# Norms on ScalarE by logarithm and exponential, and some products moved to GpSimd, in a two-layer convolution and state-space kernel

## The chip, the core and the metric

The kernel runs on one core of a Trainium2 chip. A core has TensorE (matrix products; weight loads overlap them), VectorE, ScalarE and GpSimd for work on elements, and a queue of SyncE that issues the transfers here. TensorE writes its results to PSUM, eight banks of 128 x 512 float32; the other tiles lie in SBUF. In the profile the engines are called PE (PEld for weight loads), DVE, ACT, POOL and SP. The metric is the device time of one execution in microseconds, as the median of several runs; lower is better.

## The reference

The input is x, 8 images of 64 channels by 128 by 128, float32. The first layer is a filter with a weight of its own for every pixel:

```python
h = conv3x3(x, w1) + b1;  h = where(h >= 0, h, 0.2 * h)
w_lp = softmax(conv1x1(h, w2) + b2, axis=1)        # 9 weights for each pixel
x = x + sum_k tap_k(x) * (delta_center - w_lp[k])
```

The second layer takes each image as 16,384 pixels with 64 channels:

```python
x_norm = layernorm_over_channels(x) * w + b
seq = res = layernorm(x_norm) * w + b
for i in range(2):                                  # bimamba_block
    xz = rmsnorm(seq) @ in_proj;  x, z = split(xz)  # 128 channels each
    y = mamba(x, z, forward) + mamba(x, z, backward)
    seq = seq + y @ out_proj
seq = conv3x3(rmsnorm(seq)) + res
x = x + depthwise3x3(conv1x1(x_norm)) * seq
g = depthwise3x3(conv1x1(layernorm_over_channels(x)))       # 340 channels
out = x + conv1x1(gelu(g[:170]) * g[170:])
```

One direction of `mamba` makes a causal convolution over 4 pixels with SiLU (`u`), a step `dt = softplus(...)` for each of 128 channels, and vectors B and C of 16 values for each pixel. For each channel and each of 16 states it runs over the pixels `h = exp(dt * A) * h + dt * B * u`, and sums `C * h` over the states. Every norm divides by the square root of the mean square over 64 channels plus 1e-5; there are five kinds of place for it: three in the first part of the second layer, one behind each pair of directions, and one ahead of the feed-forward part.

## The kernel before

**The scan.** A chunk is 1024 pixels of one image in one layer and one direction: 8 x 2 x 2 x 16 = 512 chunks, the class `Chunk`. Its 128 channels by 16 states are 16 tiles of 128 partitions (32 channels x 4 states) by 1024 pixels. Tile u has a slot of its own, so that a chunk has 16 slots and an image 1024. In each slot ScalarE makes the decay `exp(dt * A)` into one of two PSUM buffers `w` (`decay`, L1058), VectorE runs the recurrence (`scan`, L1076 forward and L1078 backward), and the result is multiplied by C (`product`). For each pair of tiles GpSimd makes the drive `bu` = dt * u * B (`drive`, L1050), three buffers of 128 x 2048. A product is on VectorE (L1100) or on GpSimd (L1097), as `on_pool` decides by the number of the tile: GpSimd takes the even tiles but for 4 and 12, tile 8 only beside certain other work, and none where the slot before it is that of a GELU. Where GpSimd takes it, the scan writes to `hs` in SBUF, else to `w` in PSUM. `keep` (L1090) copies the last state on ScalarE. `collect` (L1109, L1116) sums over the states on TensorE.

**The other work** is laid beside the scans. `Front` (16 pieces of 1024 pixels an image) makes the first layer and three norms; `Mix` makes the 3x3 convolutions behind the scans and one norm; `Ffn` is the feed-forward part with GELU. The next image's fronts run beside this image's third and fourth direction, the last image's mix and this one's feed-forward beside the next image's scans. The chunk of a second direction adds both directions, projects, and makes one norm.

**The order** is written out by hand. `at(time, phase, fn)` puts a step into a slot and one of six phases (FEED, SCAN, MID, PROD, DECAY, REST). The sorted list is emitted in that order, and every engine runs its own instructions in the order of the list, waiting for semaphores. So a step that waits holds up all that is behind it on its engine. The slots before the first chunk's have negative numbers; `FIRST_FRONT_AT` is the first front's.

**PSUM.** Two buffers `w` take four banks; `y`, `mm` (chunks), `bg` and `acc` (fronts, mix, feed-forward) have one bank each.

**A norm** is the class `Norm` (L406 to L430), with the square `sq` at hand:

- `means`: four matmuls with `sq` as weights and `half_mean` give the mean for each pixel, pixels on partitions, 128 x 8 in PSUM
- `means_out` (L418): ScalarE copies it to SBUF and adds epsilon
- `root` (L421): GpSimd raises it to the power -1/2
- `spread` (L427): eight matmuls with the identity put it on all 64 channels of both halves, 128 x 512 in PSUM

VectorE then multiplies by it: `scaled` (L542), `third_norm` (L574), `normed` (L1162). There are 768 norms: three in each of 128 fronts, one in each of 128 pieces of the mix, one in each of 256 chunks of a second direction.

**Table loads.** ScalarE's functions lie in sets, of which one is loaded at a time. SiLU, softplus and GELU each need another set than the exponential of the decay; the loads are put in by the compiler, ahead of the first function that needs another set.

Of the kernel before, what the change touches and what calls it, by code (L numbers as in the profile page):

```python
# [8 lines left out]
F32 = mybir.dt.float32  # L9
# [26 lines left out]
PW = W + 2  # L36
FEED, SCAN, MID, PROD, DECAY, REST = range(6)
# [8 lines left out]
LAST_MIX_STEP, LAST_MIX_AT, LAST_FFN_STEP, LAST_FFN_AT = 16, 826, 8, 1084  # L46
# [9 lines left out]
def kernel(ctx: ExitStack, tc: tile.TileContext, a: dict, out: bass.AP):  # L56
# [55 lines left out]
    neg_half = const([P, 2 * ROWS], "neg_half")  # L112
    nc.vector.memset(neg_half, -0.5)
# [4 lines left out]
    half_mean = const([P, 2], "half_mean")  # L118
    nc.vector.memset(half_mean, 0.0)
    nc.vector.memset(half_mean[0:C, 0:1], 1.0 / C)  # L120
    nc.vector.memset(half_mean[C:P, 1:2], 1.0 / C)
# [42 lines left out]


# [240 lines left out]
    class Norm:  # L406


        def means(self, ps, sq):
            self.mp = ps("ms")  # L410
            for w in range(ROWS):
                nc.tensor.matmul(  # L412
                    self.mp[:, 2 * w : 2 * w + 2], sq[:, W * w : W * w + W], half_mean, start=True, stop=True
                )

        def means_out(self):
            self.r = wk.tile([P, 2 * ROWS], F32, tag="r", name="r", bufs=4)
            nc.scalar.activation(self.r, self.mp[:, 0 : 2 * ROWS], AF.Identity, bias=eps)  # L418

        def root(self):  # L420
            nc.gpsimd.tensor_tensor(self.r, self.r, neg_half, ALU.pow)  # L421

        def spread(self, ps):
            self.rb = ps("rb")
            for w in range(ROWS):
                for h in range(2):
                    nc.tensor.matmul(  # L427
                        self.rb[C * h : C * h + C, W * w : W * w + W],
                        self.r[:, 2 * w + h : 2 * w + h + 1].to_broadcast([P, C]), ident, start=True, stop=True,
                    )  # L430
# [9 lines left out]
    class Front:  # L440
# [140 lines left out]
        def plan(self, a):  # L581
# [25 lines left out]
            at(a + 23, DECAY, self.filtered)  # L607
# [14 lines left out]
            at(a + 33, REST, lambda: n2.means(acc_tile, self.sq))  # L622
            at(a + 34, DECAY, n2.means_out)
            at(a + 34, REST, n2.root)
            at(a + 36, REST, n2.spread, acc_tile)
            at(a + 37, DECAY, self.scaled, n2)
# [21 lines left out]
    class Mix(Front):  # L648
# [40 lines left out]
        def plan(self, a):  # L689
# [15 lines left out]
            at(a + 12, REST, lambda: n1.means(bg_tile, self.sq))  # L705
            at(a + 13, DECAY, n1.means_out)
            at(a + 13, REST, n1.root)
            at(a + 16, REST, n1.spread, bg_tile)
            at(a + 17, DECAY, self.scaled, n1)
            at(a + 17, DECAY, self.norm)  # L710
# [8 lines left out]
    class Ffn:  # L719
# [174 lines left out]
    class Chunk:  # L894


        def __init__(self, i):
# [8 lines left out]
            self.beside_gelu = any(self.t0 - U <= t < self.t0 + 2 * U for t in gelu_times)  # L906
            self.prev = None
# [72 lines left out]
        def softplus(self):  # L980
            dt = self.dt
            nc.scalar.activation(dt, dt, AF.Softplus)

# [193 lines left out]
        def plan(self):  # L1177
# [81 lines left out]
    with tc.manual_schedule():  # L1259
        for key in sorted(steps):  # L1260
# [31 lines left out]
```

## Time and profile before

| | |
|---|---|
| median of 3 runs | 29687.24 us (29686.83 to 29689.91) |
| the profiled execution | 29750.91 us, its span 29749.1 us |
| VectorE busy | 27302.9 us, 92% |
| GpSimd busy | 27655.0 us, 93% |
| TensorE busy | 24131.5 us, 81% |
| ScalarE busy | 18550.1 us, 62% |
| drives on GpSimd (L1050) | 4096 of 4536 ns |
| products on GpSimd (L1097), on VectorE (L1100) | 2832 of 2358 ns, 5360 of 1225 ns |
| powers on GpSimd (L421) | 768 of 1643 ns |
| means and spreads on TensorE (L412, L427) | 891.6 and 932.8 us |
| ahead of the first scan, behind the last one | 581 and 459 us |

The profile is of one execution. A group of instructions has its busy time, the mean of one, and the engine's idle time ahead of it with what ended it. An answer over stretches gives each engine's busy time between two moments, counted from the span's start. Idle time on an engine that sets nothing costs nothing; a wait is put down to the engine whose event came last.

### The profile page before, as it was taken

The numbers are of one execution on the slowest core, as the hardware profiler recorded it, in microseconds if no ns is written. First come the engines' busy times: TensorE is split into PE (matmuls) and PEld (weight loads), VectorE is DVE, ScalarE is ACT, GpSimd is POOL, SyncE is SP. The second block draws the span as 40 slices with busy tenths as digits, with TensorE's granted clock in tenths as the row PEclk, the third lists the DMA queues.
The fourth block names the chain that finished last, engine by engine and source line by source line (L and its number), as shares of the span: only waits on it lengthen the run. The fifth ranks groups of instructions, "written<-read, shape, count | busy, mean of one in ns | idle before, by whom it ended". The sixth has DMA issues, their size and how long they took to land. (4 is left out here: it accounts for less than half of the span.)

```text
span 29749.1 us, 307276 instructions
## 1 busy us (share of the span) xinstructions
PE 24131.5 (81%) x95804; PEld 8066.2 (27%) x95804; DVE 27302.9 (92%) x17562; ACT 18550.1 (62%) x28366; POOL 27655.0 (93%) x8732
## 2 busy tenths in 40 slices
PE   7766888878888788887888788887888878888578
PEld 3211332223322233222332223222232222322123
DVE  3999999999999999999999999999999999999996
ACT  2666666666666666666666666666666666666663
POOL 2999999999999999999999999999999999999993
PEclk8777888988889888988889888998898988989789
DMA  4676677767777677776777767777676766777674
GB/s 99 219 246 218 218 233 233 238 212 222 237 232 235 211 227 236 236 231 211 231 233 237 227 213 233 234 237 222 217 233 229 242 219 220 234 231 240 212 238 124
DMA packets 2530818, 6617.94 MB, mean 222 GB/s; under 512 B 418982, under 2 KB 723382, under 8 KB 2526870
## 3 DMA queue, kind: packets, MB, share of 16 engines
q1 hardware_dynamic: 2529174, 6598.27, 69.4%
q8 instruction: 757, 12.40, 0.2%
q14 instruction: 887, 7.27, 0.1%
HBM read 5364.00 MB, written 1266.18 MB: 223 GB/s over the span
## 5 line engine op out<-in xcount | busy, mean ns | idle before, releaser
L1050 POOL TENSOR_TENSOR bu<-dup,bp 128x2048 f32<-128x2048 f32 x4096 | 18567.4, 4536 | 568.0 <-DVE w L1078 413.9
L1058 ACT ACTIVATE w<-dtp,a_neg 128x1024 f32<-128x1024 f32 x8192 | 9162.5, 1118 | 514.1 <-DVE hs L1076 318.6
L1100 DVE TENSOR_TENSOR hs<-w,cp 128x1024 f32<-128x1024 f32 x5360 | 6564.4, 1225 | 322.3 <-DMA cp<-bc_dram 90.2
L1097 POOL TENSOR_TENSOR hs<-hs,cp 128x1024 f32<-128x1024 f32 x2832 | 6677.2, 2358 | 180.4 <-ACT state L1090 116.2
L1076 DVE TENSOR_TENSOR_SCAN w<-w,state,bu 128x1024 f32<-128x1024 f32 x2677 | 6281.0, 2346 | 349.9 <-ACT w L1058 349.1
L1078 DVE TENSOR_TENSOR_SCAN w<-w,state,bu 128x1024 f32<-128x1024 f32 x2683 | 6290.8, 2345 | 312.5 <-ACT w L1058 311.9
L1116 PE MATMUL y<-hs,sel_y 128*32 128x512 f32 x32768 | 5185.5, 702 | 30.3 <-POOL hs L1097 30.0
L1090 ACT COPY state<-w 128x1 f32<-128x1 f32 x5360 | 836.7, 156 | 5064.1 <-DVE hs L1100 5028.9
L1076 DVE TENSOR_TENSOR_SCAN hs<-w,state,bu 128x1024 f32<-128x1024 f32 x1419 | 3321.0, 2340 | 55.4 <-PE y L1116 28.2
L1078 DVE TENSOR_TENSOR_SCAN hs<-w,state,bu 128x1024 f32<-128x1024 f32 x1413 | 3307.3, 2341 | 54.6 <-ACT w L1058 37.6
L1109 PE MATMUL y<-xc,dskip 128*64 128x512 f32 x4096 | 1635.9, 867 | 2009.1 <-ACT yv L1133 1334.8
L928 PE MATMUL xp<-hn,wx 128*128 128x512 f32 x4096 | 2262.7, 680 | 447.8 <-ACT xc L934 344.2
L760 PE MATMUL fp<-fw,bgw 128*128 128x512 f32 (+1 forms) x5760 | 2276.1, 642 | 66.1 <-ACT ga L807 64.7
L1116 PEld LDWEIGHTS y<-hs,sel_y 128*32 128x32 f32 x32768 | 739.0, 117 | 3492.7 <-issue 2462.8
L1090 ACT COPY state<-hs 128x1 f32<-128x1 f32 x2832 | 540.6, 191 | 1827.8 <-DVE hs L1078 929.3
L421 POOL TENSOR_TENSOR r<-r,neg_half 128x8 f32<-128x8 f32 x768 | 1261.8, 1643 | 373.9 <-ACT r L418 312.3
L934 ACT ACTIVATE xc<-xp,cbias 128x512 f32<-128x512 f32 x1024 | 696.5, 680 | 1351.3 <-PE xp L928 1351.1
L969 PE MATMUL dp<-xc,wdt 128*128 128x512 f32 x2048 | 1214.9, 677 | 362.2 <-ACT dt L976 282.0
L1058 ACT ACT_TABLE_LOAD x1134 | 1454.9, 1283 | 20.1
L766 PE MATMUL fp<-fw,bgw 64*128 64x512 f32 (+1 forms) x5760 | 1415.6, 610 | 0.0
L1006 POOL TENSOR_TENSOR dt<-dt,xc 128x1024 f32<-128x1024 f32 x512 | 1211.0, 2365 | 207.9 <-DMA dt_dram<-dt 186.4
L523 PE MATMUL acc<-t,ident 128*128 128x512 f32 x2304 | 1369.5, 679 | 4.3 <-DVE t L517 4.3
(198 smaller groups left out, 27172.3 us busy)
## 6 DMA issues: line engine op xcount, KB each, us to landing
bp<-bc_dram SPq DMA_DIRECT2D x4096, 256.0 KB, 4.1
dup<-du_dram SPq DMA_DIRECT2D x4096, 256.0 KB, 5.0
dtp<-dt_dram SPq DMA_DIRECT2D x4096, 256.0 KB, 5.0
cp<-bc_dram SPq DMA_DIRECT2D x4096, 256.0 KB, 5.0
hn<-hn_dram SPq DMA_DIRECT2D x1024, 256.5 KB, 5.0
dt_dram<-dt SPq DMA_DIRECT2D x512, 512.0 KB, 3.4
du_dram<-dt SPq DMA_DIRECT2D x512, 512.0 KB, 2.6
yf_dram<-yv SPq DMA_DIRECT2D x512, 256.0 KB, 4.5
```

Source lines behind the costliest of these rows:

```text
L760: nc.tensor.matmul(o, wpair[:, i, g, m], self.win[h][:, i : i + ROWS, 0:W], start=(i == 0), stop=False)
L766: nc.tensor.matmul(o, wlast[rows, i, g, m], self.win[h][rows, i : i + ROWS, lo : W + lo], start=False, stop=(i == 2),)
L928: nc.tensor.matmul(self.xp[h], wx[:, self.l, self.d, i, :], self.hn2[:, s.start + 2 * i : s.stop + 2 * i], start=(i == 0), stop=(i == 1),)
L1050: nc.gpsimd.tensor_tensor(bu, self.dup[self.pairs[k][1]], self.over_pair("bp", k), ALU.mult)
L1058: nc.scalar.activation(w, self.dtp[gp][:, i, :], AF.Exp, scale=a_neg[:, self.l, self.d, g, j : j + 1])
L1076: nc.vector.tensor_tensor_scan(to, w, bu, s0, ALU.mult, ALU.add)
L1078: nc.vector.tensor_tensor_scan(to[:, ::-1], w[:, ::-1], bu[:, ::-1], s0, ALU.mult, ALU.add)
L1090: nc.scalar.copy(self.column(u), h[:, T - 1 : T] if self.d == 0 else h[:, 0:1])
L1097: nc.gpsimd.tensor_tensor(hs, hs, c, ALU.mult)
L1100: nc.vector.tensor_tensor(hs, w, c, ALU.mult)
L1109: nc.tensor.matmul(self.y[C * h : C * h + C, :], dskip[:, self.l, self.d, C * gp : C * gp + C], self.xc[:, s], start=True, stop=False,)
L1116: nc.tensor.matmul(self.y[lo : lo + 32, :], sel_y, hs[:, i, s], start=False, stop=(k % 4 == 3))
```

## The change

`half_mean` (128 x 2) becomes `mean_c` (128 x 128, 1/64 within each half), so that one matmul gives the mean square on all channels at once, 128 x 512 in PSUM. ScalarE then takes the logarithm (with epsilon as its bias) and the exponential of -1/2 times it, in place in PSUM. The small copy, the power on GpSimd and the eight spreading matmuls are gone. All functions of the main loop but SiLU, softplus and GELU use one set with both exponential and logarithm; its load is issued by the kernel directly behind each of those three.

The steps of the norms get other slots. In the fronts the nine weights of the filter follow each other without a gap, the logits come a slot sooner, and the third norm's matmul comes at slot 46 where its means came at 38. The chunk's mean comes at slot 16 behind the projection's start instead of 12. The last image's feed-forward starts three slots later.

`on_pool` gives tile 4 to GpSimd in chunks of a second direction beside a front, and in chunks beside a GELU stage in which no tile is skipped for a GELU; the tile 12 stays on VectorE.

```diff
-LAST_MIX_STEP, LAST_MIX_AT, LAST_FFN_STEP, LAST_FFN_AT = 16, 826, 8, 1084
+LAST_MIX_STEP, LAST_MIX_AT, LAST_FFN_STEP, LAST_FFN_AT = 16, 826, 8, 1087
...
-    half_mean = const([P, 2], "half_mean")
...
+    mean_c = const([P, P], "mean_c")
+    nc.vector.memset(mean_c, 0.0)
+    nc.vector.memset(mean_c[0:C, 0:C], 1.0 / C)
+    nc.vector.memset(mean_c[C:P, C:P], 1.0 / C)
...
+    def exp_and_ln():
+        nc.scalar.preload_act_table_set(EXP_AND_LN)
...
-        def means(self, ps, sq):
-            self.mp = ps("ms")
-            for w in range(ROWS):
-                nc.tensor.matmul(
-                    self.mp[:, 2 * w : 2 * w + 2], sq[:, W * w : W * w + W], half_mean, start=True, stop=True
-                )
-
-        def means_out(self):
-            self.r = wk.tile([P, 2 * ROWS], F32, tag="r", name="r", bufs=4)
-            nc.scalar.activation(self.r, self.mp[:, 0 : 2 * ROWS], AF.Identity, bias=eps)
+        def mean(self, ps, sq):
+            self.rb = ps("rb")
+            nc.tensor.matmul(self.rb, mean_c, sq, start=True, stop=True)
 
         def root(self):
-            nc.gpsimd.tensor_tensor(self.r, self.r, neg_half, ALU.pow)
-
-        def spread(self, ps):
-            self.rb = ps("rb")
-            for w in range(ROWS):
-                for h in range(2):
-                    nc.tensor.matmul(
-                        self.rb[C * h : C * h + C, W * w : W * w + W],
-                        self.r[:, 2 * w + h : 2 * w + h + 1].to_broadcast([P, C]), ident, start=True, stop=True,
-                    )
+            nc.scalar.activation(self.rb, self.rb, AF.Ln, bias=eps)
+            nc.scalar.activation(self.rb, self.rb, AF.Exp, scale=-0.5)
...
-            at(b + 21, REST, self.logits)
-            at(b + 23, DECAY, self.less_max)
-            at(b + 23, DECAY, self.exps)
-            at(b + 24, DECAY, self.sums)
-            at(b + 24, REST, self.softmax)
+            at(b + 20, REST, self.logits)
+            at(b + 22, DECAY, self.less_max)
+            at(b + 22, DECAY, self.exps)
+            at(b + 23, DECAY, self.sums)
+            at(b + 23, REST, self.softmax)
...
-                t = a + k + (k >= 3)
+                t = a + k
...
-            at(a + 25, REST, lambda: n1.means(bg_tile, self.sq))
-            at(a + 26, DECAY, n1.means_out)
-            at(a + 26, REST, n1.root)
-            at(a + 28, REST, n1.spread, bg_tile)
-            at(a + 29, DECAY, self.scaled, n1)
+            at(a + 25, REST, lambda: n1.mean(bg_tile, self.sq))
+            at(a + 27, DECAY, n1.root)
+            at(a + 28, DECAY, self.scaled, n1)
...
-            at(a + 38, REST, lambda: n3.means(bg_tile, self.sq))
-            at(a + 39, DECAY, n3.means_out)
-            at(a + 39, REST, n3.root)
-            at(a + 47, REST, n3.spread, bg_tile)
-            at(a + 48, DECAY, self.third_norm)
-            at(a + 48, REST, self.store_hn)
+            at(a + 46, REST, lambda: n3.mean(bg_tile, self.sq))
+            at(a + 48, DECAY, n3.root)
+            at(a + 49, DECAY, self.third_norm)
+            at(a + 49, REST, self.store_hn)
...
+            if not self.alone:
+                exp_and_ln()
...
+            self.skips = any(self.t0 + u - 1 in gelu_times for u in (0, 8))
...
                 nc.scalar.activation(self.gt, self.gt, AF.Silu)
+            exp_and_ln()
...
             nc.scalar.activation(dt, dt, AF.Softplus)
+            exp_and_ln()
...
-            if u % 2 or u % 8 == 4 or self.t0 + u - 1 in gelu_times:
+            if u % 2 or u == 12 or self.t0 + u - 1 in gelu_times:
                 return False
+            if u == 4:
+                return self.beside_front and self.second or self.beside_gelu and not self.skips
             return u != 8 or self.beside_front or self.beside_gelu
...
-            at(b + 12, FEED, lambda: n.means(mm_tile, self.sq))
-            at(b + 13, DECAY, n.means_out)
-            at(b + 14, REST, n.root)
-            at(b + 17, FEED, n.spread, mm_tile)
+            at(b + 16, REST, lambda: n.mean(mm_tile, self.sq))
+            at(b + 17, DECAY, n.root)
             at(b + 18, DECAY, self.normed)
```

More of the change, by code (lines that the diff above doesn't have):

```diff
@@ L36 @@
 PW = W + 2
+EXP_AND_LN = "natural_log_exp_and_others"
 FEED, SCAN, MID, PROD, DECAY, REST = range(6)
@@ L111 @@
     nc.vector.memset(eps, EPS)
-    neg_half = const([P, 2 * ROWS], "neg_half")
-    nc.vector.memset(neg_half, -0.5)
     sel_y = const([P, 32, 1], "sel_y")
@@ L117 @@
     sel_y = sel_y.rearrange("k m o -> k (m o)")
-    half_mean = const([P, 2], "half_mean")
-    nc.vector.memset(half_mean, 0.0)
-    nc.vector.memset(half_mean[0:C, 0:1], 1.0 / C)
-    nc.vector.memset(half_mean[C:P, 1:2], 1.0 / C)
+    mean_c = const([P, P], "mean_c")
+    nc.vector.memset(mean_c, 0.0)
+    nc.vector.memset(mean_c[0:C, 0:C], 1.0 / C)
+    nc.vector.memset(mean_c[C:P, C:P], 1.0 / C)
     ident2 = const([P, P], "ident2")
@@ L606, in plan @@
                 at(t + 13, REST, self.gather, k)
-            at(a + 23, DECAY, self.filtered)
+            at(a + 22, DECAY, self.filtered)
             at(a + 23, REST, self.store_x1)
@@ L621, in plan @@
             at(a + 32, DECAY, self.centered_out)
[L622 to L626, printed above, removed]
+            at(a + 33, REST, lambda: n2.mean(acc_tile, self.sq))
+            at(a + 35, DECAY, n2.root)
+            at(a + 36, DECAY, self.scaled, n2)
             at(a + 37, DECAY, self.second_norm)
             at(a + 37, REST, self.store_h)
-            at(a + 38, REST, lambda: n3.means(bg_tile, self.sq))
-            at(a + 39, DECAY, n3.means_out)
-            at(a + 39, REST, n3.root)
-            at(a + 47, REST, n3.spread, bg_tile)
-            at(a + 48, DECAY, self.third_norm)
-            at(a + 48, REST, self.store_hn)
+            at(a + 46, REST, lambda: n3.mean(bg_tile, self.sq))
+            at(a + 48, DECAY, n3.root)
+            at(a + 49, DECAY, self.third_norm)
+            at(a + 49, REST, self.store_hn)
     def copy_x(b, i):
@@ L704, in plan @@
             at(a + 11, DECAY, self.centered_out)
[L705 to L710, printed above, removed]
+            at(a + 12, REST, lambda: n1.mean(bg_tile, self.sq))
+            at(a + 14, DECAY, n1.root)
+            at(a + 15, DECAY, self.scaled, n1)
+            at(a + 16, DECAY, self.norm)
             at(a + 17, REST, self.store_rows, xn_img, "hc")
@@ L1259 @@
     with tc.manual_schedule():
+        exp_and_ln()
         for key in sorted(steps):
```

## The prediction

> **What bounds the kernel now.** I read the page's busy line and groups first, then the same engines over stretches of one image, then the waits inside two of them. Ahead of the bar of a group stand line, engine, operation, operands and count; behind it busy us, mean ns of one, and idle us before it.
>
> ```profile
> PE 24131.5 (81%) x95804; PEld 8066.2 (27%) x95804; DVE 27302.9 (92%) x17562; ACT 18550.1 (62%) x28366; POOL 27655.0 (93%) x8732
> ...
> L1097 POOL TENSOR_TENSOR hs<-hs,cp 128x1024 f32<-128x1024 f32 x2832 | 6677.2, 2358 | 180.4 <-ACT state L1090 116.2
> ...
> L421 POOL TENSOR_TENSOR r<-r,neg_half 128x8 f32<-128x8 f32 x768 | 1261.8, 1643 | 373.9 <-ACT r L418 312.3
> L934 ACT ACTIVATE xc<-xp,cbias 128x512 f32<-128x512 f32 x1024 | 696.5, 680 | 1351.3 <-PE xp L928 1351.1
> ...
> L1058 ACT ACT_TABLE_LOAD x1134 | 1454.9, 1283 | 20.1
> ```
>
> Two engines are full, VectorE and GpSimd; the reader should see that 768 powers on eight columns each cost GpSimd 1262 us, more than half of a product on 1024 columns apiece. Which of the two sets the pace changes with the stage:
>
> ```profile
> core 0: us, PE busy (x) PEld busy (x) DVE busy (x) ACT busy (x) POOL busy (x), PEclk, DMA share, GB/s
> 9747.00:10428.00 681.00, 525.16 (x2073) 170.05 (x2069) 637.06 (x428) 429.29 (x678) 666.17 (x225) 0.84 0.64 209
> 10428.00:11137.00 709.00, 616.03 (x2657) 226.34 (x2658) 666.04 (x474) 464.90 (x748) 685.06 (x239) 0.89 0.72 226
> 11371.00:12027.00 656.00, 543.83 (x2042) 191.37 (x2042) 614.74 (x354) 408.95 (x615) 640.10 (x199) 0.89 0.74 234
> 12027.00:12243.00 216.00, 165.53 (x634) 45.01 (x632) 203.47 (x117) 144.60 (x209) 207.01 (x60) 0.90 0.66 221
> 12243.00:13132.00 889.00, 787.03 (x3172) 245.67 (x3168) 837.40 (x508) 587.63 (x866) 834.15 (x244) 0.92 0.73 240
> ```
>
> These are, in order: A, 12 chunks beside a front in a first direction; B, 12 beside a front in a second direction; C, 12 beside the mix, first direction; D, 4, and E, 16, beside the GELU stage, first and second direction. GpSimd is busy 97.8% of A, 96.6% of B, 97.6% of C; in E VectorE leads. The waits of GpSimd in A, then in E, say the same (total us, times, longest):
>
> ```profile
> POOL bu L1050 <- DVE w L1078: 1.2, 3, 0.4
> ```
> ```profile
> POOL bu L1050 <- DVE w L1078: 49.7, 27, 2.6
> ```
>
> In A it never waits for VectorE to free a drive buffer, so it is behind; in E it is ahead and waits. VectorE's own waits in A name ScalarE, which had waited for TensorE (`xp`), whose queue holds sums that wait for GpSimd's products: GpSimd's lateness reaches VectorE by that road.
>
> ```profile
> DVE w L1078 <- ACT w L1058: 19.1, 11, 3.2
> DVE hn L574 <- PE rb L427: 10.2, 3, 4.3
> ```
>
> **Two pages weighed.** The Trainium skill, "GPSIMD Engine Reference", section "Performance versus the Vector engine", holds elementwise work on GpSimd to be about twice as slow. The trace agrees: the state product takes 2358 ns there and 1225 ns on VectorE (group of L1100). I use the trace. "ScalarE: Activation LUTs", section "What ACT_TABLE_LOAD costs", prices each switch at about 2.66 us, 1283 ns of load and as much again of drain, and its section "Table sets" says that a set with both exponential and logarithm spares the second switch. The trace has the 1283 ns, but only 20.1 us of idle before 1134 loads, so no drain: 1.3 us per switch. The forecast goes by the trace; and by the page for this, that logarithm and exponential alternate without a load, which no row of before shows. If they did not, 1536 more loads would cost ScalarE 1971 us.
>
> **The change, part by part.** A few counts come from the instruction order: GpSimd's state products go from 2832 to 3007 (+175), powers from 768 to 0, table loads from 2273 to 2274. An engine's neighbouring instructions overlap by about 0.07 us in the timeline, so I charge a power 1.57, a product on GpSimd 2.29 and on VectorE 1.165 us.
>
> *GpSimd:* −768 × 1.57 = −1206, +175 × 2.29 = +401: −805 us in all. *VectorE:* −175 × 1.165 = −204 us. What this is worth is read by stage. The other stages' level of play: in D both engines are within 2% of each other and 9.0 us of 216 are left, 2.25 per chunk; I give that to each stage where the change levels the two.
>
> - A (97 chunks): 19 powers go, 666.2 − 31.1 = 635.1 on GpSimd; VectorE 637.1 leads. 637.1 + 27 = 664 for 681: 1.4 per chunk, 136 us.
> - B (98, each gets one product more): 35 powers go, 685.1 − 57.6 + 27.5 = 655.0; VectorE 666.0 − 14.0 = 652.0. 655 + 27 = 682 for 709: 2.25 per chunk, 221 us.
> - C (70): 640.1 − 24.9 = 615.2 against 614.7; + 27 = 642 for 656: 1.15 per chunk, 80 us.
> - E (112; one chunk in three gets a product): VectorE leads, 837.4 − 5.8; its stalls of 3.2 per chunk are GELU's and stay: 0.36 per chunk, 40 us.
> - D (70; every other chunk gets a product, and nearly no power was there to go): GpSimd leads, + 1.15 per chunk if uncovered. Half is taken, since the chunk without it lets GpSimd catch up: −40 us.
> - The last image's mix in a second direction and seven mixed chunks (26): 1.5 each, 40 us.
>
> *Ahead of the first scan* (581 us, GpSimd empty): fronts follow each other in about 47 us, bound by TensorE and by the chain of three norms. One norm's chain from square to product takes 7.5 us (341.3 to 348.8 in the timeline); without the ScalarE copy, power and eight small matmuls, with logarithm and exponential, about 2.5 less. Three norms in seven fronts: 50 us. *Behind the last scan* (459 us) only two norms are on the path, and the feed-forward's start three slots later has no clock of slots behind the scans: 5 us, either sign.
>
> *TensorE:* means 891.6 and spreads 932.8 us go; one 128x512 matmul comes, priced by the centring one (331.6 us for 256, 1.3 each): 1000. So −824 us, and no wait for GpSimd's `r` in its queue (252 us before weight loads). It is no bound, but late `xp` is what stalls ScalarE for 1351 us; part of the level play above rests on it.
>
> *ScalarE:* the logarithm with a bias pointer by L934's row, 0.68; the exponential by the 0.58 of a plain 128x512 copy; less the 0.26 of the removed Identity: +1.0 × 768 = 768 us, to 65%. PSUM to PSUM in place is in no row: 0.9 to 1.2 each are the bounds, 690 to 920 us; a saving is excluded, two passes replace one tiny one. Behind it in ScalarE's queue stand a state copy and the next decay exponential, and VectorE's scan waits for that. Two decay buffers and a scan of 2.35 us cover most of it. I let one norm in eight show in full: 100 us lost; none to all are the ends. The table load moved directly behind SiLU, softplus and GELU is hidden or not exactly as now: zero. Of the moved bank uses, the mean waits for `bc` to leave its bank, as the spread did; zero, and 0.2 us per chunk's norm (50 us) if that cover is gone. The moved logits, weights and stores issue the same matmuls and DMAs, in other slots with a slot or two of slack: zero, ±40.
>
> Sum: 136 + 221 + 80 + 40 − 40 + 40 + 50 + 5 − 100 = 432 us; the other 39 chunks have nothing of it. The profiled execution took 29750.9 (span 29749.1), 64 above the median; 29750.9 − 432 = 29319, and at the median 29687.2 − 432 = **29255 us**.
>
> **Rivals.**
> 1. *Slower: ScalarE's queue.* The root stands ahead of the decay for a later scan; if every norm delays that scan in full, and also waits for a late mean, the loss is 1.3 × 768 = 998 us against gains of 532: about 30,150. With the 1.0 alone, 768: 29,920. For it: scans already wait 661 us for decays. Against: ScalarE has a third of its time free even in B (464.9 of 709, 500 after), and of some 700 us that scans wait for decays only 57 follow a table load, which is as long a burst. It decides from 532 / 768 = 0.69 us lost per norm; taken at 29,920.
> 2. *VectorE's holes stay.* Its idle time in A to C (44, 43, 41 us) is put down to ScalarE and TensorE, not to GpSimd. If it stays, GpSimd's relief is worth nothing and only the 204 us of products come back: 29,480. Against: the road by TensorE's queue above.
> 3. *More than forecast.* TensorE's 824 us and the vanished waits for `rb` (10.2 in A, 614 us over the run) pull the holes down to 1 us per chunk: some 1.25 × 270 chunks = 340 us on top, less what is already counted: about 28,980.
> 4. *The sets do reload*, 1971 us on ScalarE: excluded by the order of loads.
>
> **How the numbers follow.** Forecast 57%, between 29,100 and 29,400; rival 2 18%, between 29,400 and 29,620; rival 3 9%; rival 1 11%; gains and losses cancelling 5%. The range, 29,030 to 29,640, leaves out rival 1 and half of rival 3. About 0.2%, 59 us, is what a measurement tells from no change: faster 0.83, same 0.06, slower 0.11.
>
> **What would show it.** No power among GpSimd's groups; its busy time near 26,850 and VectorE's near 27,100. In A and B, chunks of 55.3 and 56.8 us instead of 56.7 and 59.1, and GpSimd waiting for VectorE (`bu`) in A as it does in E. Logarithm near 680 ns and exponential near 590, with no load between them. Wrong if VectorE's waits for decays rise by more than 300 us over 661, if D lengthens by more than 1 us per chunk, or if VectorE's holes in A stay at 44 us.

## The result, and the profile after

The changed kernel takes 29782.32 us in the median of 7 runs (29765.84 to 29790.49), the kernel before 29684.84 us beside it (7 runs). The ratio is 1.0033, with a 95% interval of 1.0021 to 1.0044: slower by about 97 us, where 432 us of gain were forecast. The profiled execution of the changed kernel has a span of 29769.1 us. That is only 20 us above the span before, because the profiled execution of before lay 66 us above its median and that of the changed kernel 11 us below; the medians are compared here, and the profiles are used to see where time went.

First the page after: busy time of the engines, and the groups that answer to those shown of before (the state product on GpSimd, the decays' table loads, the eviction that waits for `xp`).

```profile
PE 23259.7 (78%) x78908; PEld 6774.1 (23%) x78908; DVE 27149.4 (91%) x17386; ACT 19315.6 (65%) x29135; POOL 26865.8 (90%) x8139
...
L1084 POOL TENSOR_TENSOR hs<-hs,cp 128x1024 f32<-128x1024 f32 x3007 | 7094.1, 2359 | 454.3 <-ACT state L1077 383.0
...
L167 ACT ACT_TABLE_LOAD x1137 | 1458.8, 1283 | 21.4 <-PEq L1267 0.7
L917 ACT ACTIVATE xc<-xp,cbias 128x512 f32<-128x512 f32 x1024 | 695.4, 679 | 1149.6 <-PE xp L911 1146.4
```

The work moved as it was counted: GpSimd 26866 us (26,850 forecast), VectorE 27149 (27,100), ScalarE 19316 against 18550, 766 us more (768 forecast), TensorE 872 us less (824). VectorE's busy time falls by 153 us and not by the 204 that moved, since its other work takes 49 us longer (27351.6 us in the changed kernel with the products as before). No group of powers is left, and the loads of tables are 2274 for 2273, as long as before. The two new passes of ScalarE, by its groups:

```profile
L418 ACT ACTIVATE rb<-rb,eps 128x512 f32<-128x512 f32 x768 | 500.5, 652 | 235.5 <-PE rb L415 234.5
L419 ACT ACTIVATE rb<-rb 128x512 f32<-128x512 f32 x768 | 447.0, 582 | 24.2
```

652 and 582 ns where 680 and 590 were taken, and 24 us of idle ahead of 768 exponentials: no table load lies between. The counts and nearly all durations of the forecast held, and the sum was wrong. The same chunks as in the stretches of before (A, B, C, D, E in this order) show it:

```profile
9689.00:10366.00 677.00, 504.62 (x1657) 141.48 (x1659) 638.43 (x428) 449.04 (x698) 637.77 (x207) 0.84 0.65 211
10366.00:11079.00 713.00, 577.78 (x1900) 172.38 (x1892) 653.10 (x461) 496.40 (x780) 660.57 (x217) 0.90 0.69 225
11309.00:11975.00 666.00, 528.80 (x1708) 167.51 (x1706) 613.23 (x352) 423.75 (x632) 620.30 (x185) 0.90 0.72 231
11975.00:12190.00 215.00, 163.14 (x628) 44.28 (x626) 202.22 (x116) 145.02 (x209) 208.96 (x61) 0.88 0.66 221
12190.00:13096.00 906.00, 775.58 (x2859) 218.03 (x2860) 834.74 (x504) 603.84 (x879) 824.28 (x235) 0.91 0.71 236
```

In A GpSimd's busy time (the fifth of the busy times) falls from 666 to 638 us, and the stretch only from 681 to 677; GpSimd does wait for VectorE there now, for 22.6 us where it was 1.2. B has 25 us less of GpSimd and 13 less of VectorE and is 4 us longer; C is 10 and E 17 us longer. Relief turned into idle time. Where, say the waits of GpSimd over the whole run (total us, times, longest):

```profile
POOL bu L1037 <- DVE w L1065: 679.9, 371, 4.0
...
POOL bu L1037 <- DVE w L1063: 395.5, 285, 3.7
POOL hs L1084 <- ACT state L1077: 383.0, 364, 10.9
```

GpSimd now waits 1075 us for VectorE to free a drive buffer (530 before) and 383 us for ScalarE's state copies (116). VectorE's own waits, before and then after:

```profile
DVE w L1076 <- ACT w L1058: 349.1, 306, 3.2
DVE hc L542 <- PE rb L427: 321.7, 121, 15.1
DVE w L1078 <- ACT w L1058: 311.9, 189, 3.2
...
DVE hn L1162 <- PE rb L427: 156.8, 80, 19.3
DVE hn L574 <- PE rb L427: 135.4, 67, 6.7
```

```profile
DVE w L1063 <- ACT w L1045: 432.8, 396, 5.1
DVE hc L531 <- ACT rb L419: 365.4, 191, 23.0
DVE w L1065 <- ACT w L1045: 317.4, 296, 3.2
DVE hn L1149 <- ACT rb L419: 237.8, 154, 17.8
```

The scans that write to `w` wait 750 us for decays (661 before). The products with a norm wait for ScalarE's exponential where they waited for TensorE's spread: with the third norm (93.2 us) 696 us, where they waited 614. Between the first and the last scan VectorE's idle time, added up from the trace, went from 1783 to 2039 us. So VectorE lost 153 us of work and gained 256 us of holes; ahead of the first scan 76 us were won.

### The profile page after: what moved, and what is told of

Same layout as the page of the kernel before. It is cut to its first block, busy times and chain, and to the rows that moved or that the text cites. A ratio compares the mean times of both kernels' runs of the same rounds, so it can differ in the third digit from the quotient of the medians.

```text
span 29769.1 us, 273090 instructions
## 1 busy us (share of the span) xinstructions
PE 23259.7 (78%) x78908; PEld 6774.1 (23%) x78908; DVE 27149.4 (91%) x17386; ACT 19315.6 (65%) x29135; POOL 26865.8 (90%) x8139
## 5 line engine op out<-in xcount | busy, mean ns | idle before, releaser
L1084 POOL TENSOR_TENSOR hs<-hs,cp 128x1024 f32<-128x1024 f32 x3007 | 7094.1, 2359 | 454.3 <-ACT state L1077 383.0
L1087 DVE TENSOR_TENSOR hs<-w,cp 128x1024 f32<-128x1024 f32 x5185 | 6349.6, 1225 | 258.8 <-DMA cp<-bc_dram 25.6
L1065 DVE TENSOR_TENSOR_SCAN w<-w,state,bu 128x1024 f32<-128x1024 f32 x2634 | 6174.2, 2344 | 322.7 <-ACT w L1045 317.4
L1063 DVE TENSOR_TENSOR_SCAN w<-w,state,bu 128x1024 f32<-128x1024 f32 x2551 | 5982.2, 2345 | 434.9 <-ACT w L1045 432.8
L1103 PE MATMUL y<-hs,sel_y 128*32 128x512 f32 x32768 | 5117.0, 694 | 85.2 <-POOL hs L1084 84.3
L1063 DVE TENSOR_TENSOR_SCAN hs<-w,state,bu 128x1024 f32<-128x1024 f32 x1545 | 3619.2, 2343 | 111.6 <-PE y L1103 57.3
L1065 DVE TENSOR_TENSOR_SCAN hs<-w,state,bu 128x1024 f32<-128x1024 f32 x1462 | 3424.7, 2343 | 78.2 <-ACT w L1045 56.2
L911 PE MATMUL xp<-hn,wx 128*128 128x512 f32 x4096 | 2176.3, 657 | 400.9 <-ACT xc L917 325.7
L953 PE MATMUL dp<-xc,wdt 128*128 128x512 f32 x2048 | 1303.3, 722 | 517.6 <-ACT dt L960 479.2
L415 PE MATMUL rb<-sq,mean_c 128*128 128x512 f32 x1536 | 977.0, 721 | 860.9 <-ACT bc L979 311.8
```

The costliest lines, as they stand in the source:

```text
L911: nc.tensor.matmul(self.xp[h], wx[:, self.l, self.d, i, :], self.hn2[:, s.start + 2 * i : s.stop + 2 * i], start=(i == 0), stop=(i == 1),)
L1063: nc.vector.tensor_tensor_scan(to, w, bu, s0, ALU.mult, ALU.add)
L1065: nc.vector.tensor_tensor_scan(to[:, ::-1], w[:, ::-1], bu[:, ::-1], s0, ALU.mult, ALU.add)
L1084: nc.gpsimd.tensor_tensor(hs, hs, c, ALU.mult)
L1087: nc.vector.tensor_tensor(hs, w, c, ALU.mult)
L1103: nc.tensor.matmul(self.y[lo : lo + 32, :], sel_y, hs[:, i, s], start=False, stop=(k % 4 == 3))
```

## The experiments

Each kernel was timed beside the kernel before on the same chip, and the median of before lies between 29,685 and 29,716 us from one such pairing to the next. So the last column, the median against that of before beside it, is what is compared; below, a time against the kernel before is always this column, while the expectations name absolute times. "Passes" are the logarithm and the exponential.

| run | median us | ratio to before, 95% interval | against before, us |
|---|---|---|---|
| changed kernel | 29782.32 | 1.0033 (1.0021 to 1.0044) | +97 |
| before, no power | 29716.51 | 1.0007 (0.9999 to 1.0016) | +20 |
| changed, products as before | 29807.87 | 1.0039 (1.0024 to 1.0054) | +111 |
| changed, no passes | 29315.00 | 0.9872 (0.9858 to 0.9887) | −382 |
| changed, table load later | 29795.69 | 1.0034 (1.0023 to 1.0046) | +99 |
| changed, multiply later | 29767.85 | 1.0022 (1.0013 to 1.0031) | +69 |
| changed, exponential only | 29606.85 | 0.9968 (0.9956 to 0.9980) | −92 |
| changed, three passes | 30273.84 | 1.0192 (1.0175 to 1.0209) | +575 |
| changed, affine passes on GpSimd | 29699.18 | 0.9993 (0.9984 to 1.0001) | −17 |
| changed, chunk's root later | 29759.01 | 1.0015 (1.0008 to 1.0021) | +43 |
| no passes, products as before | 29293.23 | 0.9856 (0.9840 to 0.9873) | −422 |
| the same, matmul twice | 29632.82 | 0.9972 (0.9961 to 0.9984) | −78 |
| affine and squares on GpSimd | 29654.62 | 0.9980 (0.9972 to 0.9989) | −56 |
| extra products dropped | 29794.45 | 1.0031 (1.0019 to 1.0042) | +95 |
| affine and squares on GpSimd, products as before | 29745.21 | 1.0014 (1.0008 to 1.0021) | +46 |

### Is GpSimd the pace?

```diff
         def root(self):
-            nc.gpsimd.tensor_tensor(self.r, self.r, neg_half, ALU.pow)
+            pass
...
-            nc.scalar.activation(self.sq, self.cp, AF.Square)
+            nc.scalar.activation(self.sq, self.cp, AF.Copy, bias=0.5, scale=0.0)
```

> The kernel before with the power on GpSimd left out, so that the norm multiplies by the mean itself; so that the numbers stay tame, the square on ScalarE is replaced by a pass of equal length that writes 0.5. The norms are thus not computed. GpSimd loses 768 x 1.57 = 1206 us of work and nothing is added anywhere. If GpSimd sets the pace beside fronts and mix, as the prediction had it, this gives at least the 440 us that A, B and C were to give: about 29,250 or less. If VectorE's holes come from the queues of ScalarE and TensorE (rival 2), only the shortened chain shows: 29,550 to 29,690.

Measured: +20 us, the interval takes in no change. The kernel before, with 1196 us less on GpSimd by the trace and nothing added, is not faster, not even by the little that the second expectation left to the shortened chain. The norms' false values changed nothing either. GpSimd's groups in that run:

```profile
L1050 POOL TENSOR_TENSOR bu<-dup,bp 128x2048 f32<-128x2048 f32 x4096 | 18579.4, 4538 | 1317.6 <-DVE w L1078 680.3 <-DVE w L1076 476.8 <-PE wb L513 70.0
L1097 POOL TENSOR_TENSOR hs<-hs,cp 128x1024 f32<-128x1024 f32 x2832 | 6679.5, 2359 | 459.2 <-ACT state L1090 350.2 <-DVE hs L1100 71.0 <-DMA cp<-bc_dram 23.9
```

The idle time ahead of the drives grew from 568 to 1318 us, with VectorE's release of the buffer at the end of it. On an engine 93% busy, the busiest of the page, this work had been no bound. The Trainium skill, "Perfetto Trace Analysis", section "Identifying the Most-Contended Engine", says to look for the engine of highest occupancy and to optimize that one first; here the measurement decides against it.

### The products

```diff
-            if u % 2 or u == 12 or self.t0 + u - 1 in gelu_times:
+            if u % 2 or u % 8 == 4 or self.t0 + u - 1 in gelu_times:
                 return False
-            if u == 4:
-                return self.beside_front and self.second or self.beside_gelu and not self.skips
```

> The changed kernel with the choice of products of the kernel before: tile 4 stays on VectorE everywhere, 2832 products on GpSimd. If the extra products cost more than the 204 us that they take from VectorE (the cover of a decay is shorter where the tile's product isn't on VectorE, and the drives come later), this is faster than the changed kernel by 50 to 200 us: 29,580 to 29,730. If the loss sits in the norms alone, it is slower than the changed kernel by up to 200 us: 29,780 to 29,980.

+111 against +97, at the lower end of the second expectation: the extra products are worth 14 us, less than the intervals can tell. The same pair without the passes (below) has −422 without them and −382 with them. Since the products moved, a gain on VectorE might have been lost again on GpSimd, so they were also dropped altogether, without the factor C:

```diff
             if self.on_pool(u):
-                nc.gpsimd.tensor_tensor(hs, hs, c, ALU.mult)
+                if u != 4:
+                    nc.gpsimd.tensor_tensor(hs, hs, c, ALU.mult)
```

> The changed kernel with the 175 extra products of tile 4 left out altogether, neither on GpSimd nor on VectorE: that tile's states are summed there without the factor C. Changed kernel 29,782 to 29,790; with the 175 products back on VectorE 29,808. If VectorE's 204 us are a gain that GpSimd's 401 us and the longer way of the product take back, this is faster than the changed kernel by 100 to 200 us: 29,580 to 29,690. If work on VectorE does not set the time here, within 50 us of it: 29,740 to 29,830.

+95, the second expectation. Against the changed kernel (+97) GpSimd has its 401 us less, and against the products on VectorE (+111) VectorE has its 204 us less: neither difference is clear of the intervals. The traces say where VectorE's part went. A hole is idle time of VectorE; added up between the first and the last scan, in us:

| kernel | scans wait for decays | VectorE waits for a norm | all of VectorE's holes |
|---|---|---|---|
| before | 703 | 431 | 1783 |
| changed | 834 | 490 | 2039 |
| changed, products as before | 700 | 483 | 1867 |
| changed, no passes | 847 | 76 | 1658 |
| no passes, products as before | 708 | 66 | 1436 |
| the same, matmul twice | 718 | 286 | 1754 |
| changed, multiply later | 1201 | 7 | 2039 |

The extra products, not the passes, lengthen the waits for decays: 700 to 834 us with the passes, 708 to 847 without. That fits what the first expectation of the products' run reasoned, that the cover of a decay is shorter where the tile's product isn't on VectorE. VectorE's holes grow by 172 us for the 202 us of work that it is spared.

### The two passes on ScalarE

```diff
         def root(self):
-            nc.scalar.activation(self.rb, self.rb, AF.Ln, bias=eps)
-            nc.scalar.activation(self.rb, self.rb, AF.Exp, scale=-0.5)
+            pass
...
-            nc.scalar.activation(self.sq, self.cp, AF.Square)
+            nc.scalar.activation(self.sq, self.cp, AF.Copy, bias=0.5, scale=0.0)
```

> The changed kernel with logarithm and exponential left out, so that VectorE multiplies by the mean out of the matmul; the square writes 0.5 as in the run without power. The norms are thus not computed. ScalarE loses 947 us. If their place in ScalarE's queue eats the gain (rival 1), this reaches what was forecast without the 100 us for them, about 29,150 to 29,300. If the holes have another cause (TensorE's queue, the products), it stays at 29,600 to 29,780.

−382, a little above the first expectation: the passes cost 479 us, about half of the 947 us that they take, or 0.62 us for each of 768 norms. The values that stand in for the norm are those of the run without power, which was no faster for them. With one pass and with three it becomes a series. One pass, in the run just shown:

```diff
         def root(self):
-            pass
+            nc.scalar.activation(self.rb, self.rb, AF.Exp, scale=-0.5)
```

> The changed kernel with the logarithm left out and the exponential kept, and the square writing 0.5 as in the run without both; the norms are not computed. ScalarE's part of the chain is 0.58 us instead of 1.23. Without both passes the time was 29,315, with both 29,782 to 29,796. If the loss is a delay, it grows about in proportion: 29,520 to 29,600. If it is the hand-over from TensorE by ScalarE to VectorE, whatever the length, most of it is there with one pass: 29,680 to 29,780.

Three passes, in the changed kernel:

```diff
             nc.scalar.activation(self.rb, self.rb, AF.Exp, scale=-0.5)
+            nc.scalar.copy(self.rb, self.rb)
```

> The changed kernel with a third pass on ScalarE, a plain copy of the norm onto itself in PSUM, 0.58 us for each of 768 norms (445 us). If each added pass delays VectorE by about its share of what the first two did (470 us for 1.23 us), this costs 220 us: 29,960 to 30,060. If what is lost is the hand-over, or is covered by then, it costs under 80 us: 29,780 to 29,860. If every pass is felt in full, 445: 30,200.

| passes | us on ScalarE for a norm | against before, us | step, us | passes added by the step, us | wait for a norm, us | scans' wait for decays, us |
|---|---|---|---|---|---|---|
| none | 0 | −382 | | | 76 | 847 |
| exponential | 0.57 | −92 | 290 | 436 | 256 | 854 |
| and logarithm | 1.23 | +97 | 189 | 512 | 490 | 834 |
| and copy | 1.80 | +575 | 478 | 438 | 832 | 859 |

The exponential alone lands just above the range of "in proportion", and the third pass is felt in full, its last expectation. It is not one hand-over that costs, but every pass: 957 us for 1386 us of passes, on the mean 0.69 us for each us. In the traces the cost stands as VectorE's wait for the norm itself; the waits for decays stay as they were. The mean granted clock of TensorE falls along the series too, 0.891, 0.883, 0.879 and 0.872, and its busy time for the same matmuls rises from 23,044 to 23,480 us; the most frequent matmul, of `y`, took 689, 695, 694 and 692 ns, without a trend. Whether part of the cost came by way of the clock is not shown.

### Which wait is it?

The forecast charged the passes for decays that come late behind them, and the table above shows no such delay. The products with a norm wait 603 us for it in the two largest of their lines shown above (479 before). So it seemed that the norm is read too early, and its reader was moved.

```diff
-            at(a + 28, DECAY, self.scaled, n1)
+            at(a + 29, DECAY, self.scaled, n1)
...
-            at(a + 15, DECAY, self.scaled, n1)
-            at(a + 16, DECAY, self.norm)
+            at(a + 16, DECAY, self.scaled, n1)
+            at(a + 17, DECAY, self.norm)
...
-            at(b + 18, DECAY, self.normed)
+            at(b + 19, DECAY, self.normed)
```

> The changed kernel with VectorE's multiplication a slot further behind the logarithm and exponential: n1 at slot 29, n2 at 37, the mix at 16, the chunk at 19; for n3 the matmul at 45, the root at 46 and the multiplication at 48, so that its bank is free before the next front's mean; the maximum of the logits a slot sooner and the sums of the softmax a slot later; the chunk's load of h and the last feed-forward one slot later. Same work on every engine. If what VectorE loses is the wait for a norm that isn't there yet (490 us in the changed kernel, and 114 for the softmax's exponential), most of it goes: 29,250 to 29,500, better than both. If the log and exp hold VectorE by delaying the decays behind them, moving the reader changes nothing: 29,720 to 29,830.

+69, 28 us better and within the intervals of no difference. VectorE's waits in that run:

```profile
DVE w L1063 <- ACT w L1045: 646.8, 450, 4.4
DVE w L1065 <- ACT w L1045: 477.4, 317, 3.2
DVE t L506 <- PE wb L502: 281.7, 185, 20.1
DVE mx L462 <- PE lp L456: 256.2, 127, 47.3
```

The wait for the norm is gone (7 us are left between the first and last scan, of 490), and in these two rows the scans' wait for decays has grown from 750 to 1124 us. VectorE's holes there are 2039 us in both kernels. My theory, that moving the reader alone brings the time back, fell: most of the wait went to the next readers of ScalarE, the scans, which fits a ScalarE that runs late. It is not the whole of it. Between the scans VectorE's wait at the maximum of the logits (`mx`) rose from 13 to 187 us, and this edit itself had put the maximum a slot sooner. What the later multiplication would do without that move was not run.

Two more changes of its place. The table load put ahead of the next user instead of behind SiLU, softplus and GELU:

```diff
     def exp_and_ln():
-        nc.scalar.preload_act_table_set(EXP_AND_LN)
+        Tables.stale = True
+
+    def want_exp():
+        if Tables.stale:
+            Tables.stale = False
+            nc.scalar.preload_act_table_set(EXP_AND_LN)
...
             w = pw.tile([P, T], F32, tag="w", name="w")
+            want_exp()
```

`want_exp` also stands ahead of the logarithm and of the softmax's exponential.

> The changed kernel with the load of the joint table set issued ahead of the next function that needs it, as the kernel before has it, instead of directly behind SiLU, softplus and GELU: state copies and evictions between the two come before the load again. If the early load delays the state copies that GpSimd's products wait for (383 us against 116), and that matters, this is faster than the changed kernel by 50 to 150 us: 29,630 to 29,730. If not, within 30 us of it: 29,750 to 29,810.

+99: no difference, the second expectation. But GpSimd's wait for state copies did not fall (412 us against 383), so the early load was not its cause, and this run does not tell what that wait is worth. And the chunk's norm behind the softplus instead of ahead of it:

```diff
-            at(b + 16, REST, lambda: n.mean(mm_tile, self.sq))
-            at(b + 17, DECAY, n.root)
-            at(b + 18, DECAY, self.normed)
+            at(b + 18, REST, lambda: n.mean(mm_tile, self.sq))
+            at(b + 19, DECAY, n.root)
+            at(b + 20, DECAY, self.normed)
```

> The changed kernel with the chunk's mean, root and product at slots 18, 19 and 20 instead of 16, 17 and 18: away from the copy of B and C ahead of it and behind the softplus with its two table loads (3.6 us) instead of before it; the load of h and the projection come later for the bank. If the burst of ScalarE's work around the softplus, with the root added, is what VectorE waits for, the third of the loss that sits in these 256 norms falls: 29,600 to 29,720. If lateness only moves to the next reader, as when the product was moved, no change: 29,750 to 29,830.

29,759, which by itself is the second expectation; but the kernel before was at 29,716 beside it, and +43 is 54 us better than the changed kernel. The two intervals touch at 1.0021, so a gain is possible and not shown. In its trace the waits for a norm fall from 490 to 309 us, and VectorE's holes hardly (2039 to 2026).

### ScalarE's load itself

```diff
-            nc.scalar.activation(self.h0, self.h0, AF.Identity, bias=vec["pe_norm_b"], scale=vec["pe_norm_w"])
+            nc.gpsimd.tensor_scalar(self.h0, self.h0, vec["pe_norm_w"], vec["pe_norm_b"], ALU.mult, ALU.add)
...
-            nc.scalar.activation(self.hc, self.hc, AF.Identity, bias=vec["norm2_b"], scale=vec["norm2_w"])
+            nc.gpsimd.tensor_scalar(self.hc, self.hc, vec["norm2_w"], vec["norm2_b"], ALU.mult, ALU.add)
...
-            nc.scalar.activation(self.hn, self.hn, AF.Copy, scale=vec["normf_w"])
+            nc.gpsimd.tensor_scalar(self.hn, self.hn, vec["normf_w"], None, ALU.mult)
```

> The changed kernel with three of ScalarE's passes given to GpSimd, which has about 1100 us of idle more than before: scale and bias of the second norm of the front and of the mix's norm, and the last layer's weights (384 passes, 299 us of ScalarE); the square for the third norm and the stores come later for it, the softmax's sums a slot later. If it is ScalarE's own load that makes it late for VectorE, at the slope of the other runs (0.4 to 1 us for 1 us) this gives 110 to 300 us: 29,490 to 29,680. If it is the place of the norm alone, or GpSimd's longer queue costs as much, within 60 us of the changed kernel: 29,720 to 29,850.

−17, 114 us better than the changed kernel, as the first expectation had it (29,699 by itself lies between the two). ScalarE is busy for 254 us less, so each us of it gave about 0.45 (0.2 to 0.7 by the intervals), though GpSimd got 379 us more. Some steps got other slots as well, which no run takes apart. With the squares too, and the chunk's later norm:

```diff
-            nc.scalar.activation(self.sq, self.op, AF.Square)
+            nc.gpsimd.tensor_tensor(self.sq, self.h, self.h, ALU.mult)
```

> The run with three affine passes on GpSimd, with the chunk's norm two slots later as in the run before, and with two of the three squares (the chunk's, 256, and the one for the third norm, 128) as products on GpSimd too, the chunk's from the copy of h: 535 us less on ScalarE than in the changed kernel, about 490 us more on GpSimd. The full result is computed. The first 299 us gave 90 us and the later norm 25; at the same slope the squares give 70: 29,560 to 29,660, faster than the kernel before. If GpSimd, then at some 27,750 us busy, becomes the late one, 29,700 or more.

−56, ratio 0.9980 (0.9972 to 0.9989), within the first expectation: this version computes everything and beats both kernels, by 0.2 and 0.5%. Its lead on the run with the affine passes alone (−17) lies within the intervals. GpSimd is at 93% again, as before the change. Whether that holds it up was asked by giving it the choice of products of before, by the same edit as above:

```diff
-            if u == 4:
-                return self.beside_front and self.second or self.beside_gelu and not self.skips
```

> The run with affine passes and squares on GpSimd (29,655), with the products as in the kernel before: 401 us less on GpSimd, which is at 27,624 us there, 204 more on VectorE. The full result is computed. If GpSimd has become the late one in that run, 29,500 to 29,610; if neither engine's total matters, within 50 us: 29,610 to 29,700.

+46, slower by 102 us, a result that neither expectation had. In that version the place of the products does count: VectorE has 197 us more work and 102 us less of holes. The 392 us less on GpSimd again bring nothing that shows.

### What was won, and where

What is left when the passes and the extra products are taken out is one matmul for means and spreads, no copy and no power, in the new slots and with the early table load.

```diff
         def root(self):
-            nc.scalar.activation(self.rb, self.rb, AF.Ln, bias=eps)
-            nc.scalar.activation(self.rb, self.rb, AF.Exp, scale=-0.5)
+            pass
...
-            if u % 2 or u == 12 or self.t0 + u - 1 in gelu_times:
+            if u % 2 or u % 8 == 4 or self.t0 + u - 1 in gelu_times:
                 return False
-            if u == 4:
-                return self.beside_front and self.second or self.beside_gelu and not self.skips
```

> The run without logarithm and exponential, and with the products as in the kernel before, so that only the one matmul for means and spreads, the missing copy and power, and the slots are left of the change (norms not computed). Without the two passes, with the new products, it was 29,315. If the 175 products are worth VectorE's 204 us once ScalarE is in time, this is at 29,480 to 29,560. If they are worth as little as in the full kernel (26 us), 29,320 to 29,380, and the shorter chain is worth 340 us by itself.

−422, below both expectations and nearer the second: what is left is worth 422 us by itself, and the products are worth nothing beside it. By the table of waits it is the norm that comes in time: VectorE's holes fall from 1783 to 1436 us, and its wait for a norm from 431 to 66. Which part of the change does it? The power by itself was worth nothing, by the first run. Work on TensorE was put back:

```diff
             nc.tensor.matmul(self.rb, mean_c, sq, start=True, stop=True)
+            nc.tensor.matmul(self.rb, mean_c, sq, start=True, stop=True)
```

> The run without logarithm and exponential and with the products as before (29,293), with the mean's matmul made twice, the second over the first: 768 x 1.27 = 976 us of TensorE more, about what the change takes from TensorE. Norms not computed. If the 403 us that this run gains on the kernel before come from TensorE's relief, they are gone by half or more: 29,490 to 29,700. If they come from the hand-overs that fall away (copy on ScalarE, power on GpSimd, spread), it stays within 80 us: 29,280 to 29,370.

−78, the first expectation: 344 of the 422 us are gone, for second matmuls that are busy for 884 us (TensorE's busy time rises by 660 us in all). The wait of ScalarE for `xp` and for `bcp` (idle time ahead of the instruction, and what ended it) in the run without the second matmul, then with it:

```profile
L917 ACT ACTIVATE xc<-xp,cbias 128x512 f32<-128x512 f32 x1024 | 695.8, 680 | 1092.1 <-PE xp L911 1088.9
...
L979 ACT COPY bc<-bcp 64x512 f32<-64x512 f32 x512 | 296.1, 578 | 543.3 <-PE bcp L972 443.9 <-PE y L1101 96.4
```
```profile
L918 ACT ACTIVATE xc<-xp,cbias 128x512 f32<-128x512 f32 x1024 | 696.7, 680 | 1208.8 <-PE xp L912 1204.8
...
L980 ACT COPY bc<-bcp 64x512 f32<-64x512 f32 x512 | 296.1, 578 | 651.2 <-PE bcp L973 536.3 <-PE y L1102 111.5
```

ScalarE waits 224 us longer in these two rows. VectorE's wait for the chunk's norm, without and with:

```profile
DVE hn L1147 <- PE rb L416: 93.6, 55, 19.1
```
```profile
DVE hn L1148 <- PE rb L417: 314.1, 155, 19.1
```

So the time hangs on what TensorE does for the norm, with TensorE at 79%. Two ways are open. The second matmul loads TensorE, but it also stands in the norm's own chain, just ahead of its reader, and 220 of the 319 us that VectorE's holes grow by are the wait for that norm; those put down to ScalarE stay (986 and 993 us). The same matmul somewhere off the chain was not run, so that TensorE's load by itself is worth this much is not shown. The mean granted clock is 0.893 in both, so it is no matter of that; it is 0.879 in the kernel before.

In steps from the kernel before to the changed one: −422 for the norm by one matmul, +533 for the two passes (from −422 to +111 with the products as before), −14 for the products. They add up to +97 because each starts where the last one ends, which is no test of the account.

## Why the prediction was wrong

- **"GpSimd is the pace in A, B and C" (437 us, in a sum of 432).** This step failed. The power's removal is worth nothing (+20 us) where 440 were to come. That GpSimd was busy 97.8% of A and waited hardly ever for a buffer only says that it was just in time; VectorE's holes in the same stretch named ScalarE and TensorE, and the forecast explained them away by a road from GpSimd through TensorE's queue that was only argued. The "level play" built on it, 2.25 us per chunk, has no meaning where neither of the two engines sets the time. A slip on top is small: B and C take a power at 1.64 us and not at the 1.57 charged above, which makes their gain some 30 us too large.
- **"VectorE, −204 us".** Worth nothing clear in the changed kernel: the same products on VectorE give +111, on GpSimd +97, dropped +95. The work turned into waits for decays. Rival 2, "the holes stay", was right for GpSimd and wrong in its own 204 us.
- **"I let one norm in eight show in full: 100 us lost".** This term was mis-sized: the passes cost 479 us (with the new products) to 533 (with the old), 0.62 to 0.69 us for a norm. Rival 1 had a loss of this size, and 0.69 as its point of decision, but by the same wrong road: both have the decay late behind the root. The waits for decays do not change with the passes (847 and 834 us); the wait for the norm itself rises from 76 to 490. That ScalarE is late for other reasons when the root comes, 1146 us of waiting for `xp` among them, would fit this and is not shown.
- **"It is no bound" of TensorE's 824 us.** Too little on the other side: without passes and extra products the rest of the change gives 422 us, and a second matmul for each norm takes 344 of them. The forecast gave TensorE a share in the "level play" and no line of its own in the sum. Rival 3 had it: holes pulled down by some 340 us; without passes and extra products VectorE's holes fall by 347. That the two figures are so close may be chance.
- **The signs.** No sign of being wrong came as it was named: the waits for decays rose by 89 us in the rows meant, D is 1 us shorter, and VectorE's holes in A went from 44 to 39. But they went from 43 to 60 in B and from 41 to 53 in C, which no sign watched. GpSimd's waiting in A came as forecast and brought nothing with it.
- **Right:** the counts, both durations, the loads; that the early table load is worth nothing; the end (459 to 454 us); the start better by 76 us for 50. In stage D the loss did not come: its 4 chunks are 1 us shorter, where some 2 us more were forecast.

## What to carry to other kernels

With engines that each run a fixed list and wait for each other, a busy share, even 93%, does not say that an engine sets the time: before trading work between engines, leave the work out on the one to be relieved, and see if the time moves at all. Price a pass by what the others' holes name, here ScalarE and TensorE at 62 and 81%: in this kernel a us of the passes on ScalarE cost 0.4 to 1.1 us, a us of the doubled matmul 0.4, and GpSimd's powers and products nothing that shows. A wait that vanishes when its reader is moved may not be won; see whether the next reader waits longer.

## What the runs showed of the hardware that was not expected

On GpSimd, scale and bias together took half the time of the scale alone, on 128 x 512 elements in place with the factors from SBUF. By its groups in the fastest version that computes everything:

```profile
L1149 POOL TENSOR_TENSOR sq<-h 128x512 f32<-128x512 f32 x256 | 269.3, 1052 | 3.3 <-ACT h L1142 3.3
L1156 POOL TENSOR_SCALAR hn<-hn,v_normf_w 128x512 f32<-128x512 f32 x128 | 201.2, 1572 | 2.8 <-DVE hn L1153 2.0 <-issue 0.8
...
L673 POOL TENSOR_SCALAR hc<-hc,v_norm_w,v_norm_b 128x512 f32<-128x512 f32 x128 | 99.6, 778 | 18.7 <-DVE hc L531 17.4 <-DMA xmw<-xm_dram 1.2
```

778 ns with two operations and 1572 ns with one (773 and 1567 in the run with the affine passes alone); a square of a tile by itself takes 1052 ns, and a sum of two tiles 1275. What makes the single operation slow is open. The dose of passes is not even either: the third pass, of 570 ns, cost 478 us where the logarithm, of 652 ns, cost 189, and why is open.
